# Narrow pieces of an attention row maximum: a plain maximum on VectorE, with the mask added on TensorE

## The chip, the cores and the metric

The kernel runs on one core of a Trainium2 chip. The metric is the device time of one execution in microseconds (us), taken as the median of several runs. The engines named below are TensorE (PE in the profile, its weight loads PEld), VectorE (DVE), ScalarE (ACT), GpSimd (POOL) and the DMA queue of SyncE (SP).

## The reference

The computation is one transformer layer over x of shape 4 x 1024 x 256, with a context of 77 rows per batch element placed in front of the keys. Attention has 16 heads of 16 numbers, and a query may see the whole context and the x rows up to its own:

```
xc = concatenate((mem, layernorm(x)))          # 77 + 1024 = 1101 keys
q, k, v = heads(layernorm(x) @ Wq), heads(xc @ Wkv)
dots = (q @ k.T) * 16 ** -0.5
dots = where(key > query + 77, -inf, dots)     # the triangle
x = x + softmax(dots) @ v @ Wout + bout
x = x + ffn(layernorm(x))                      # 256 -> 1024 -> gelu -> 256, block-quantized operands
```

The softmax is computed with the largest score of each row subtracted, so that row maximum has to be known before the exponentials. Everything in this document is about how that maximum is found.

## The kernel before

The 64 pairs of batch element and head are worked off in 16 groups `kk` of four heads. Within a group the four heads c = 0 to 3 lie in four bands of 32 partitions of the tiles `qTs` and `kTs`. A band holds the 16 numbers of the head, and one row more, into which the negated row maximum is written, so that the matmul of scores subtracts it by itself.

Each group passes through two phases, and the phases of neighbouring groups are interleaved: while the scores of group kk are computed, turned into exponentials and multiplied by v, the row maxima of group kk + 1 are found. The unit of this interleaving is `half_step(kk, n, pair)`. In it TensorE does two matmuls for the maxima (`max_matmul`, L523, into a tile of the pool `ps_s`, which has three buffers) and two for the scores (`score_matmul`, L587, into `ps_st`, two buffers), alternating, each on its own band of 32 rows of the array, so that they run beside each other. The trace shows each of these float32 matmuls as two passes, so that such a block has eight rows. Then VectorE takes the maxima of the two tiles (`max_reduce`), and ScalarE takes the exponentials (`score_exp`, L598). After the half-step come the products with v of an earlier step (`times_v`, L624), and then the units of other work (layer norm, projections, the feed-forward part, loads) which a planner by prices and due times fits in. All engines work off their instructions in the order in which they were written, and the three `ps_s` buffers are shared by the maxima and all those units: a matmul that needs a buffer waits until VectorE or ScalarE has read what was in it.

The keys that a tile of 128 queries can see are cut into pieces (`max_pieces`). For query tile `it` there are 77 + 128 (it + 1) keys. The widths of the pieces, in the order in which they are worked off, are

| query tiles | pieces by width |
|---|---|
| it 0 to 3 | 512 (it 3), 461 (it 2), 333 (it 1), 205 (it 0), 77 (it 3) |
| it 4 to 7 | 512 (it 4, 5, 6, and two of it 7), 461 (it 6), 333 (it 5), 205 (it 4), 77 (it 7) |

A piece that ends at the tile's own last key is diagonal: its last 128 columns hold the triangle. The pieces of 205 columns are diagonal, those of 77 are not. `max_reduce` has two forms. A first piece that is not diagonal is read by `tensor_reduce` (L547). Every other piece is read by a custom operation (`tensor_tensor_reduce`, L549; CUSTOM_DVE_ANT_0 in the profile). It adds a mask from the float32 tile `tri` (zeros, or the triangle in the last 128 columns), takes the maximum, starting from the result `mx` of the row's earlier piece where there is one, and writes the sums to a scrap tile `jk`. It is followed by a short instruction that reads out the result (DVE_READ_ACCUMULATOR2_ANT). For a piece of 77 columns the mask is all zeros.

The results are columns of the tile `mxp`, one tile for even and one for odd groups. `put_max` transposes it (L557) and sends it through DRAM into the maximum row of `qTs`, once for each half of the query tiles. Group 0 has no earlier group beside it: `first_step` does the maxima of its four heads at once, two of them in a `ps_st` tile.

Of the kernel before, what the change touches and what calls it, by code (L numbers as in the profile page):

```python
# [9 lines left out]
F32 = mybir.dt.float32  # L10
BF16 = mybir.dt.bfloat16
I32 = mybir.dt.int32
AF = mybir.ActivationFunctionType
ALU = mybir.AluOpType
AX = mybir.AxisListType
PSUM = bass.MemoryType.PSUM

P = 128
HEADS = 16
HD = 16  # L20
PAD = 32
HPC = P // HD
MXR = 1
HPG = 4
NG = HEADS // HPG
ICW = 512
# [17 lines left out]
def kernel(  # L44
# [14 lines left out]
    nc = tc.nc  # L59
    B, N, D = x.shape  # L60
    M = mem.shape[1]
    HID = w_fc.shape[0]
    NT = N // P
# [8 lines left out]
    const = ctx.enter_context(tc.tile_pool(name="const", bufs=1))  # L72
    small = ctx.enter_context(tc.tile_pool(name="small", bufs=4))
# [9 lines left out]
    for w, src in ((wk_sb, wkv[:, 0:D]), (wq_sb, wq), (wv, wkv[:, D : 2 * D]), (wo_sb, wout)):  # L83
# [6 lines left out]
    ZW = ICW - P  # L90
    tri = const.tile([P, ICW], F32, name="tri")
# [2 lines left out]
        out=tri[:, ZW:], in_=tri[:, ZW:], compare_op=ALU.is_ge, fill=NEG, base=0,  # L94
        pattern=[[-1, P]], channel_multiplier=1,
    )
    ones3 = const.tile([3, P], BF16, name="ones3")
    nc.gpsimd.memset(ones3, 1.0)

# [3 lines left out]
    identb = const.tile([P, P], BF16, name="identb")  # L103
# [126 lines left out]
    with ExitStack() as actx:  # L230
        ap = lambda name, bufs, **kw: actx.enter_context(tc.tile_pool(name=name, bufs=bufs, **kw))
        keep = ap("keep", 1)
# [13 lines left out]
        junk = ap("junk", 4)  # L246
# [18 lines left out]
            "q": keep.tile([P, N], F32, name="q_st"), "k": keep.tile([P, KEYS], F32, name="k_st")  # L265
        }
        mxps = [keep.tile([P, 2 * HPG * NT // 2], F32, name=f"mxp{i}") for i in range(2)]
        for i in range(2):
            nc.gpsimd.memset(mxps[i], 0.0)
        for i in range(2):  # L270
            nc.gpsimd.memset(qTs[i], 0.0)
        zero = keep.tile([P, 1], F32, name="zero")
# [18 lines left out]
        def s_tile(shape, dtype=F32):  # L291
            return ps_s.tile(shape, dtype, tag="s", name="s_ps")
# [206 lines left out]
        def max_pieces():  # L499

            pieces = []
            for half in range(NIC):
                some = []
                for it in range(half * ICW // P, (half + 1) * ICW // P):
                    n = M + (it + 1) * P
                    full, left = divmod(n, ICW)

                    lo = left if left < P else 0  # L510
                    cuts = [(lo + i * ICW, lo + (i + 1) * ICW) for i in range(full)]
                    if left:
                        cuts.append((0, left) if lo else (n - left, n))
                    some += [(it, *c, i, len(cuts)) for i, c in enumerate(cuts)]
                pieces += sorted(some, key=lambda p: p[1] - p[2])
            return pieces

        mxs = {}

        def max_matmul(kk, piece, c, sp):  # L520
            it, lo, hi, _, _ = piece
            rows = slice(c * PAD, (c + 1) * PAD)
            nc.tensor.matmul(  # L523
                sp[:, 0 : hi - lo], qTs[kk % NQK][rows, it * P : (it + 1) * P],
                kTs[kk % NQK][rows, lo:hi],
                start=True, stop=True,
            )

        def max_reduce(kk, piece, c, sp):
            it, lo, hi, i, many = piece  # L530
            w = hi - lo
            if i == 0:
                before = -3.0e38
            else:
                before = mxs[kk, it, c][:, i - 1 : i]
            if i == many - 1:
                col = (it // 4 * HPG + c) * 4 + it % 4
                into = mxps[kk % 2][:, col : col + 1]
            else:
                if i == 0:  # L540
                    mxs[kk, it, c] = small.tile([P, 2], F32, name="mx", bufs=6 * HPG)
                into = mxs[kk, it, c][:, i : i + 1]
            diagonal = hi == M + (it + 1) * P
            assert diagonal or w <= ZW or i == 0
            mask = tri[:, ICW - w : ICW] if diagonal else tri[:, 0:w]
            if i == 0 and not diagonal:
                nc.vector.tensor_reduce(into, sp[:, 0:w], axis=AX.X, op=ALU.max)  # L547
            else:
                nc.vector.tensor_tensor_reduce(  # L549
                    junk.tile([P, ICW], BF16, name="jk")[:, 0:w], sp[:, 0:w], mask, 1.0, before, ALU.add, ALU.max, into  # L550
                )

        def put_max(kk, half):


            mt = small.tile([P, PAD], F32, name="mt")
            nc.vector.transpose(mt, mxps[kk % 2])  # L557
            NQ, NI = P // PAD, ICW // P
            md = dram.tile([NQ, 2, HPG, NI, PAD], F32, name="md")
            nc.sync.dma_start(out=md.rearrange("q f c i j -> (q f c i) j"), in_=mt)  # L560
            nc.sync.dma_start(
                out=qTs[kk % NQK][MXR:P:PAD, half * ICW : (half + 1) * ICW].rearrange(
                    "c (i q j) -> c i q j", q=NQ, j=PAD
                ),
                in_=md[:, half].rearrange("q c i j -> c i q j"),
            )
# [16 lines left out]
        def score_matmul(kk, n, c, st, e):  # L583
            t, ic, i0, i1 = PIECES[n]
            nj = min(P, KEYS - t * P)
            rows = slice(c * PAD, (c + 1) * PAD)
            nc.tensor.matmul(  # L587
                st[:nj, e, : i1 - i0], kTs[kk % NQK][rows, t * P : t * P + nj],
                qTs[kk % NQK][rows, i0:i1],
                start=True, stop=True,  # L590
            )

        def score_exp(kk, n, pair, st):
            t, ic, i0, i1 = PIECES[n]
            nj = min(P, KEYS - t * P)
            w = i1 - i0
            pt = ptp.tile([P, 2, ICW], F32, name="pt")
            nc.scalar.activation(pt[:nj, :, :w], st[:nj, :, :w], AF.Exp, scale=scale)  # L598

            base = i0 - (t * P - M)  # L600
            behind = min(w, nj - 1 - base)
            if behind > 0:
                nc.gpsimd.affine_select(  # L603
                    out=pt[:nj, :, :behind], in_=pt[:nj, :, :behind], compare_op=ALU.is_ge,
                    fill=0.0, base=base, pattern=[[0, 2], [1, behind]], channel_multiplier=-1,
                )
            pts[kk, n, pair] = pt
# [321 lines left out]
        MAXP = max_pieces()  # L929
# [67 lines left out]
        def first_step(n):  # L997

            st = ps_st.tile([P, 2, ICW], F32, name="st_ps")
            tops = [s_tile([P, ICW]), s_tile([P, ICW]), st[:, 0, :], st[:, 1, :]]  # L1000
            for c, sp in enumerate(tops):
                max_matmul(0, MAXP[n], c, sp)
            for c, sp in enumerate(tops):
                max_reduce(0, MAXP[n], c, sp)

        def half_step(kk, n, pair):

            other = 1 - pair
            tops, st = [], None
            has_max, has_main = kk + 1 < B * NG, kk >= 0  # L1010
            if has_main:
                st = ps_st.tile([P, 2, ICW], F32, name="st_ps")
            for e in range(2):
                if has_max:
                    tops.append(s_tile([P, ICW]))
                    max_matmul(kk + 1, MAXP[n], pair * 2 + e, tops[e])
                if has_main:
                    score_matmul(kk, n, other * 2 + e, st, e)
            for e, sp in enumerate(tops):
                max_reduce(kk + 1, MAXP[n], pair * 2 + e, sp)  # L1020
            if has_main:
                score_exp(kk, n, other, st)
# [10 lines left out]
        def run(kk, extras):  # L1033
# [10 lines left out]
            for n in range(STEPS):  # L1044
                for pair in range(2):
                    if kk == last:
                        if pair == 0:
                            last_step(kk, n)
                    elif kk >= 0:
                        half_step(kk, n, pair)  # L1050
                    elif pair == 0:
                        first_step(n)
# [5 lines left out]
                    if n == 1 and pair == 0 and kk >= 0:  # L1058
                        put_max(kk, 1)
                    if n == HALF_AT + 2 and pair == 0 and kk + 1 < B * NG:  # L1060
                        put_max(kk + 1, 0)
# [31 lines left out]
        for kk in range(last + 1):  # L1093
            b, g = divmod(kk, NG)
            f = b - 1
# [35 lines left out]
            else:  # L1131
                n = -(-len(w_units) // NG)
# [60 lines left out]
```

## Time and profile before

| what | value |
|---|---|
| median of three runs | 1026.15 us (1023.31 to 1030.79) |
| time of the profiled execution | 1026.0 us |
| its span, first to last instruction | 1024.3 us |
| mean granted TensorE clock in it | 0.962 |
| busy: PE, PEld, DVE, ACT, POOL | 958.9, 406.9, 651.7, 564.9, 363.2 us |

The span is cut into 40 slices in the profile, and PE is busy in 90% or more of each from the third to the 37th. The clock was granted in full from 60 us to 905 us, but for a rounding. A busy time of PE is a union of pipelined instructions whose ends are modelled, so it is read together with the starts of the instructions in the timeline. A row of a group of instructions gives line, engine, operation, tiles written and read, shapes, count, then busy time and the mean of one instruction in ns, then the idle time of the engine in front of them and what ended it.

### The profile page before, as it was taken

The numbers are of one execution on the slowest core, as the hardware profiler recorded it, in microseconds if no ns is written. First come the engines' busy times: TensorE is split into PE (matmuls) and PEld (weight loads), VectorE is DVE, ScalarE is ACT, GpSimd is POOL, SyncE is SP. The second block draws the span as 40 slices with busy tenths as digits, with TensorE's granted clock in tenths as the row PEclk, the third lists the DMA queues.
The fourth block names the chain that finished last, engine by engine and source line by source line (L and its number), as shares of the span: only waits on it lengthen the run. The fifth ranks groups of instructions, "written<-read, shape, count | busy, mean of one in ns | idle before, by whom it ended". The sixth has DMA issues, their size and how long they took to land.

```text
span 1024.3 us, 21081 instructions
## 1 busy us (share of the span) xinstructions
PE 958.9 (94%) x8015; PEld 406.9 (40%) x8024; DVE 651.7 (64%) x2131; ACT 564.9 (55%) x838; POOL 363.2 (35%) x763
## 2 busy tenths in 40 slices
PE   4899999999999999999999999999999999999477
PEld 2343434344444343334443444334443444344133
DVE  4586776677667565647567475646558486662696
ACT  4234665555555655666555665665555665766134
POOL 1011323041435254333625244434425246342133
PEclk9899999999999999999999999999999999989566
DMA  3012000401021001200121001100122000002100
GB/s 106 23 54 67 10 29 8 112 14 40 27 70 26 17 10 36 80 7 27 31 69 38 19 15 36 40 7 16 32 66 58 12 13 14 17 8 74 47 21 21
DMA packets 36172, 36.31 MB, mean 35 GB/s; under 512 B 14067, under 2 KB 29747, under 8 KB 36070
## 3 DMA queue, kind: packets, MB, share of 16 engines
q1 hardware_dynamic: 34958, 33.90, 12.0%
q8 instruction: 63, 1.03, 0.4%
q10 hardware_dynamic: 1112, 1.06, 0.3%
q14 instruction: 39, 0.32, 0.1%
HBM read 16.58 MB, written 5.25 MB: 21 GB/s over the span
## 4 chain that ended last, share of the span: by engine, by line
PE 79%; DVE 11%; ACT 3%; DMA 2%; issue 2%; POOL 1%; SPq 1%; POOLq 0%; DVEq 0%; ACTq 0%
PE s_ps L523 33%; PE av_ps L624 16%; PE s_ps L446 6%; PE st_ps L587 5%; DVE jk L549 4%; PE st_ps L810 3%; PE s_ps L417 3%; PE s_ps L725 3%; PE s_ps L870 2%; PE st_ps L815 2%; DVE mx L547 1%; PE s_ps L862 1%; ACT pt L598 1%; DVE amaxh L183 1%; ACT h L821 1%
## 5 line engine op out<-in xcount | busy, mean ns | idle before, releaser
L598 ACT ACTIVATE pt<-st_ps 128x1024 f32<-128x1024 f32 (+4 forms) x448 | 353.2, 793 | 261.6 <-PE st_ps L587 237.4
L523 PE MATMUL s_ps<-kT,qT 32*128 32x512 f32 (+2 forms) x1736 | 481.1, 529 | 13.4 <-DVE mxp L549 5.8
L587 PE MATMUL st_ps<-qT,kT 32*128 32x512 f32 (+5 forms) x1792 | 472.8, 526 | 3.3 <-ACT pt L598 3.0
L603 POOL TENSOR_SCALAR_AFFINE_SELECT pt<-pt 128x254 f32<-128x254 f32 (+3 forms) x320 | 118.0, 371 | 422.8 <-ACT pt L598 422.1
L523 PEld LDWEIGHTS s_ps<-kT,qT 32*128 32x128 f32 x1736 | 188.4, 184 | 188.9 <-issue 66.1
L549 DVE CUSTOM_DVE_ANT_0 jk<-s_ps,tri,mx 128x77 bf16<-128x77 f32 (+3 forms) x372 | 174.0, 505 | 90.2 <-PE st_ps L587 58.8
L624 PE MATMUL av_ps<-pt,vaug 128*32 128x256 f32 (+7 forms) x3072 | 221.1, 362 | 2.1 <-issue 0.6
L547 DVE TENSOR_REDUCE mx<-s_ps 128x1 f32<-128x512 f32 x248 | 159.3, 684 | 88.5 <-PE st_ps L587 84.5
L549 DVE CUSTOM_DVE_ANT_0 jk<-s_ps,tri 128x512 bf16<-128x512 f32 (+3 forms) x248 | 126.9, 549 | 130.6 <-PE st_ps L587 95.7
L587 PEld LDWEIGHTS st_ps<-qT,kT 32*128 32x128 f32 (+1 forms) x1792 | 182.2, 181 | 12.9 <-ACT pt L598 9.4
L624 PEld LDWEIGHTS av_ps<-pt,vaug 128*32 128x32 f32 (+1 forms) x3072 | 61.9, 108 | 190.7 <-issue 128.2
L206 POOL TENSOR_TENSOR hq<-h,magh 128x512 bf16<-128x512 f32 x64 | 68.7, 1077 | 32.9 <-DVE h L205 29.8
L205 POOL TENSOR_TENSOR h<-h,magh 128x512 f32<-128x512 f32 x40 | 41.9, 1049 | 53.7 <-DVE magh L194 53.7
L821 ACT ACTIVATE h<-st_ps 128x1024 f32<-128x1024 f32 x32 | 32.8, 1025 | 30.3 <-PE st_ps L815 30.2
L183 DVE TENSOR_REDUCE amaxh<-h 128x16 f32<-128x512 f32 x64 | 42.7, 677 | 8.9 <-ACT h L821 8.9
L710 ACT COPY y<-s_ps 128x256 f32<-128x256 f32 x64 | 23.9, 374 | 42.9 <-PE s_ps L729 22.5
L810 PE MATMUL st_ps<-wfcT,xqT 128*128 128x512 bf16 x119 | 41.5, 428 | 3.1 <-ACT xqT L791 2.9
L549 DVE DVE_READ_ACCUMULATOR2_ANT mxp<- 128x1 f32 x512 | 42.1, 82 | 0.0
L417 PE MATMUL s_ps<-wv,xT 128*128 128x256 f32 (+1 forms) x144 | 40.8, 409 | 0.3 <-ACT vaug L422 0.3
L446 PE MATMUL s_ps<-xT,wk_sb 128*128 128x512 f32 (+1 forms) x96 | 38.8, 532 | 0.0
L870 PE MATMUL s_ps<-wprT,hT 128*128 128x256 bf16 x256 | 35.8, 286 | 3.2 <-ACT hT L865 2.6
L725 PE MATMUL s_ps<-wo_sb,o_pk 128*128 128x256 f32 x128 | 38.8, 429 | 0.0
(105 smaller groups left out, 797.7 us busy)
## 6 DMA issues: line engine op xcount, KB each, us to landing
kT<-k_st SPq DMA_DIRECT2D x16, 275.2 KB
xn<-in_x_dram SPq DMA_DIRECT2D x16, 256.0 KB
qT<-q_st SPq DMA_DIRECT2D x16, 256.0 KB
o_pk<-o_st SPq DMA_DIRECT2D x32, 128.0 KB
rb<-rd SPq DMA_DIRECT2D x128, 32.0 KB
x<-in_x_dram SPq DMA_DIRECT2D x32, 128.0 KB
out_dram<-x SPq DMA_DIRECT2D x32, 128.0 KB
x<-in_L_ffn_w_fc_dram SPq DMA_DIRECT2D x8, 128.0 KB
```

The costliest lines, as they stand in the source:

```text
L206: nc.gpsimd.tensor_tensor(dst.rearrange("p (n k) -> p n k", k=QBLK), src3, magb, ALU.subtract)
L417: nc.tensor.matmul(vp[:nj, :], xT[b][:, k, jt * P : jt * P + nj], wv[:, k, :], start=(k == 0), stop=(k == KC - 1),)
L446: nc.tensor.matmul(pp[:, :n], w[:, k, hi * P : (hi + 1) * P], xT[b][:, k, first + lo : first + lo + n], start=(k == 0), stop=(k == KC - 1),)
L523: nc.tensor.matmul(sp[:, 0 : hi - lo], qTs[kk % NQK][rows, it * P : (it + 1) * P], kTs[kk % NQK][rows, lo:hi], start=True, stop=True,)
L547: nc.vector.tensor_reduce(into, sp[:, 0:w], axis=AX.X, op=ALU.max)
L549: nc.vector.tensor_tensor_reduce(junk.tile([P, ICW], BF16, name="jk")[:, 0:w], sp[:, 0:w], mask, 1.0, before, ALU.add, ALU.max, into)
L587: nc.tensor.matmul(st[:nj, e, : i1 - i0], kTs[kk % NQK][rows, t * P : t * P + nj], qTs[kk % NQK][rows, i0:i1], start=True, stop=True,)
L598: nc.scalar.activation(pt[:nj, :, :w], st[:nj, :, :w], AF.Exp, scale=scale)
L603: nc.gpsimd.affine_select(out=pt[:nj, :, :behind], in_=pt[:nj, :, :behind], compare_op=ALU.is_ge, fill=0.0, base=base, pattern=[[0, 2], [1 ...
L624: nc.tensor.matmul(acc[c * PAD : (c + 1) * PAD, off + lo : off + hi], vaugs[b % 2][:nj, t, v0 : v0 + PAD], pts[kk, n, c // 2][:nj, c % 2, ...
L725: nc.tensor.matmul(yp, o_pk[b, ic][:, k, it * P % ICW : it * P % ICW + P], wo_sb[:, k, :], start=(k == 0), stop=False,)
L810: nc.tensor.matmul(hp[:, n, :], xqT[t][:, k, :], wfcT[:, k, n * ICW : (n + 1) * ICW], start=(k == 0), stop=False,)
```

## The change

Pieces under 256 columns (those of 205 and of 77) are read by `tensor_reduce` in place of the custom operation. Since `tensor_reduce` adds no mask, a new function `max_mask` lets TensorE add the triangle to the last 128 columns of a diagonal narrow piece: a bf16 matmul of the identity with `trib`, a bf16 copy of the triangle, which accumulates into the tile that `max_matmul` filled. It stands behind all matmuls of the half-step. Pieces of 77 columns get no mask.

The maximum of a narrow piece no longer starts from that of the row's other piece. It goes into its own column of a new tile `mxn` (where it is the row's only piece, it 0, into `mxp`), and `put_max` takes the larger of `mxp` and `mxn` with one operation on 16 columns before it transposes. The custom operation stays for the diagonal pieces of 333, 461 and 512 columns. The order of all other instructions on every engine's queue stays as it was.

```diff
+    trib = const.tile([P, P], BF16, name="trib")
+    nc.vector.tensor_copy(trib, tri[:, ZW:])
...
+        mxns = [keep.tile([P, 2 * HPG * NT // 2], F32, name=f"mxn{i}") for i in range(2)]
         for i in range(2):
             nc.gpsimd.memset(mxps[i], 0.0)
+            nc.gpsimd.memset(mxns[i], -3.0e38)
...
+        NARROW = 256
+
+        def masked(piece):
+            it, lo, hi, _, _ = piece
+            return hi == M + (it + 1) * P and hi - lo < NARROW
+
+        def max_mask(piece, sp):
+            it, lo, hi, _, _ = piece
+            if masked(piece):
+                nc.tensor.matmul(
+                    sp[:, hi - lo - P : hi - lo], identb, trib, start=False, stop=True,
+                    skip_group_check=True,
+                )
+
         def max_reduce(kk, piece, c, sp):
             it, lo, hi, i, many = piece
             w = hi - lo
...
+            col = (it // 4 * HPG + c) * 4 + it % 4
+            into, beside = (m[kk % 2][:, col : col + 1] for m in (mxps, mxns))
             diagonal = hi == M + (it + 1) * P
...
+            if w < NARROW:
+                assert masked(piece) or not diagonal
+                nc.vector.tensor_reduce(
+                    beside if many > 1 else into, sp[:, 0:w], axis=AX.X, op=ALU.max
+                )
+                return
+            wide = [p for p in MAXP if p[0] == it and p[2] - p[1] >= NARROW]
+            i = [p[1] for p in wide].index(lo)
+            if i < len(wide) - 1:
+                mxs[kk, it, c] = small.tile([P, 1], F32, name="mx", bufs=6 * HPG)
+            target = into if i == len(wide) - 1 else mxs[kk, it, c]
...
         def put_max(kk, half):
+            part = slice(half * PAD // 2, (half + 1) * PAD // 2)
+            nc.vector.tensor_tensor(
+                mxps[kk % 2][:, part], mxps[kk % 2][:, part], mxns[kk % 2][:, part], ALU.max
+            )
             mt = small.tile([P, PAD], F32, name="mt")
             nc.vector.transpose(mt, mxps[kk % 2])
...
         def half_step(kk, n, pair):
...
+            for sp in tops:
+                max_mask(MAXP[n], sp)
             for e, sp in enumerate(tops):
                 max_reduce(kk + 1, MAXP[n], pair * 2 + e, sp)
```

## The prediction

> **What bounds the kernel now.** I read the engines' totals first, then the slices, then the chain that ended last. All three stand on the profile's page.
>
> ```profile
> PE 958.9 (94%) x8015; PEld 406.9 (40%) x8024; DVE 651.7 (64%) x2131; ACT 564.9 (55%) x838; POOL 363.2 (35%) x763
> ...
> PE   4899999999999999999999999999999999999477
> ...
> PE 79%; DVE 11%; ACT 3%; DMA 2%; issue 2%; POOL 1%; SPq 1%; POOLq 0%; DVEq 0%; ACTq 0%
> ```
>
> PE is the bound: its 65 us without work lie mostly at the two ends, and the slices from the third to the 37th, where nearly all maxima are found, are full. VectorE is 11% of the chain, so here and there PE does wait for it. The view of waits says where: PE's weight loads for the maxima (L523) wait for VectorE to give back a buffer.
>
> ```profile
> PEld s_ps L523 <- DVE mxp L549: 46.1, 119, 1.7
> PEld s_ps L523 <- DVE mx L547: 28.1, 61, 1.0
> PEld s_ps L523 <- DVE mx L549: 12.9, 31, 0.8
> ```
>
> That is 87 us over 211 waits, but other bands often work meanwhile. What is lost I read from the timeline as the time from a block's first matmul to the next work. A block with nothing to wait for takes 0.56 us at 205 columns and 0.38 at 77; over all 62 and 63 blocks of these widths the means are 0.66 and 0.54. So the narrow blocks lose 62 x 0.10 + 63 x 0.16 = 16 us in all. This is the most that faster narrow maxima could give back in their own steps.
>
> **The masks on TensorE.** Groups 1 to 15 have their maxima in half-steps; each has four half-steps of 205 columns (two query tiles, two pairs), each with two masks: 60 pairs, 120 matmuls. Group 0 has two steps with four masks. Before shows no mask, but it shows a near twin: L788 turns two 128 x 128 bf16 tiles with the same identity, each with its own weight load. In the timeline of TensorE:
>
> ```profile
> 330.78 0.28 PE L788 MATMUL s_ps<-identb,xq 128*128 128x128 bf16 x2
> 331.00 0.54 PE L523 MATMUL s_ps<-kT,qT 32*128 32x333 f32 x1
> ...
> 336.22 0.44 PE L523 MATMUL s_ps<-kT,qT 32*128 32x205 f32 x1
> ...
> 336.77 0.60 PE L624 MATMUL av_ps<-pt,vaug 128*32 128x231 f32 x8
> ...
> 363.95 0.62 PE L862 MATMUL s_ps<-identb,hq 128*128 128x128 bf16 x8
> 364.50 0.69 PE L523 MATMUL s_ps<-kT,qT 32*128 32x512 f32 x1
> ```
>
> The pair holds TensorE 0.215 us from its start to the next block's (0.22 here; 0.215 is the commonest over all such pairs), eight hold it 0.55 us. The slope is (0.55 - 0.215) / 6 = 0.056 us a matmul, and 0.10 us is paid once, for going from the full array back to bands. A block of 205 columns takes its 0.56 us before the products with v, and blocks in front of full-array work take no longer (1.07 us at 512 columns before L870 as before L624), so a mask pair between them adds the whole 0.215. Sixty pairs are 12.9 us; group 0's two sets are 2 x (4 x 0.056 + 0.10) = 0.65. Sum: **+13.5 us**, on the engine that sets the end. Bounds: 128 x 0.056 = 7 us if the change of kind is free, since both neighbours pay for it already; and 13.5 + 128 x 0.10 = 26 us if each weight load is laid bare (0.10 us is the mean of L862's and L788's loads). I take the pair as measured; the accumulation into a filled bank is new, but L810, which accumulates too, shows no gap for it.
>
> The Trainium skill, "TensorE: Matmul & The Clock Gate", section "Back-to-back issue gap", gives 134 cycles at 2.4 GHz, 56 ns, for an isolated matmul of 128 columns; the slope agrees, and by this alone 128 masks would be 7.2 us. The 0.10 us for the change of kind is not in that formula, and for it the rows decide.
>
> **The narrow maxima on VectorE.** The rows by shape, and two stretches of VectorE's timeline:
>
> ```profile
> L547 DVE TENSOR_REDUCE mx<-s_ps 128x1 f32<-128x512 f32 x248 | 159.3, 684 | 88.5 <-PE st_ps L587 84.5 <-PE st_ps L523 2.7 <-PE s_ps L523 0.5
> L549 DVE CUSTOM_DVE_ANT_0 jk<-s_ps,tri,mx 128x77 bf16<-128x77 f32 x124 | 32.2, 295 | 27.8 <-PE s_ps L523 21.1 <-PE st_ps L587 5.5
> L183 DVE TENSOR_REDUCE amaxx<-xh 128x8 f32<-128x256 f32 x32 | 13.2, 413 | 0.0
> ```
>
> ```profile
> 494.41 0.43 DVE L549 CUSTOM_DVE_ANT_0 jk<-s_ps,tri,mx 128x205 bf16<-128x205 f32 x1
> 494.76 0.08 DVE L549 DVE_READ_ACCUMULATOR2_ANT mxp<- 128x1 f32 x1
> ...
> 517.32 0.30 DVE L549 CUSTOM_DVE_ANT_0 jk<-s_ps,tri,mx 128x77 bf16<-128x77 f32 x1
> 517.54 0.08 DVE L549 DVE_READ_ACCUMULATOR2_ANT mxp<- 128x1 f32 x1
> ...
> 519.02 1.29 DVE L547 TENSOR_REDUCE mx<-s_ps 128x1 f32<-128x512 f32 x2 [0.71 <-PE st_ps L587]
> ```
>
> The custom operation and the reading of its result overlap the next one: what counts is the step from start to start, 0.35 us for 205 columns that start from mx (494.41 to 494.76), 0.29 us for 205 without it, and 0.22 us for 77. Two plain maxima of 512 columns take 1.29 us, each alone 0.68, so their step is 0.61. The plain maximum costs (677 - 413) / 256 = 1.03 ns a column (L183 at 512 and at 256 columns), which puts its step at 0.61 - 435 x 0.00103 = 0.16 us for 77 columns and 0.29 us for 205. So VectorE gains 128 x 0.06 for the 77s, 64 x 0.06 for it 4, and nothing for it 0: 11.5 us. The bounds are no gain at all, if the step has a floor at the 0.22 of the custom one, and 256 x 0.08 = 20 us, if every reading of a result (82 ns) went in full. `put_max` gets 32 operations on 16 columns, and the transpose waits for each: the small operations of L162 stand 0.20 us apart, so +6.4 us, between 32 x 0.17 and 32 x 0.40. The balance is some -5 us of VectorE's 652.
>
> How much reaches PE? Sorted by what they wait for, about half of the narrow blocks' 16 us goes to VectorE working off a queue that other work has lengthened (statistics, quantization), the rest mostly to ScalarE and GpSimd. In some 20 such blocks the shorter maxima (two to four in front of the waiting matmul, 0.06 each) give back about 0.15 us each: -3 us. In another nine or so PE would have waited anyway behind a mask pair, for ScalarE or GpSimd, and the pair fits in: -2 us. Against this, `put_max` falls into the steps of 461 and 512 columns, where PE waits for VectorE most; I let a sixth of its 6.4 us through: +1 us. Sum: **-4 us**, between -16 (all waits of narrow blocks gone) and +6 (nothing gained, all of `put_max` let through).
>
> The Trainium skill speaks against the new operation: "VectorE: DVE Perf Modes", section "Rules for kernel authors", calls tensor_reduce the slowest VectorE operation. Here it takes 684 ns at 512 columns against 689 to 748 for the custom one, so the rule does not hold for this pair; by it the gain would be nothing, which is the lower bound above.
>
> **What costs nothing.** The copy into `trib` stands first on VectorE and waits for GpSimd's triangle (2.19 us); its successors feed ScalarE at 4.17 us, and the first statistics start at 4.53, so it has 1.9 us of cover, and without it would cost at most 0.5. The two extra fills of `mxn` on GpSimd are 0.09 us each, far ahead of any reader. A masked maximum now waits for the mask, 0.1 to 0.2 us later; behind it on VectorE wait the other maximum and the planner's operations, but the products with v (0.53 us) stand on PE in between before the buffer is asked for, and they move along. ScalarE waits for the scores, which stand ahead of the masks. The transfers of `put_max` start 0.2 us later; the only DMA wait on L523 is for group 0's qT.
>
> **The forecast.** 1026.0 (profiled execution; the median is 1026.15, no difference that matters) + 13.5 - 4 = **1035.5**, 0.9% slower. A change under 1%, 10 us, can hardly be told from none here.
>
> **Rivals.**
> - *The masks' price as measured, small relief* (1030 to 1041): chance 0.5.
> - *VectorE really was the narrow steps' bound*: the masks cost only their columns (+7) and all 16 us of narrow waits go: 1017, range 1012 to 1029, chance 0.15. For it: 211 waits on VectorE. Against: most of them stand at 333 to 512 columns, and VectorE idles before most blocks of 205. It ends faster than before if the waits given back exceed the masks' price; at the measured price that takes 13.5 of the 16.
> - *The identity's weights are not loaded beside the blocks in bands*, as the full array's are needed at once: 26 - 4 = +22, 1048, range 1041 to 1054, chance 0.2. It decides once a mask pair holds PE over 0.3 us. Against: L788's loads, 0.10 us each, hide within the 0.215 us.
> - *The plain maximum is no faster when narrow* (the change doesn't do what it is for): +13.5 for the masks, +1 for `put_max`, and only the 2 us of masks that fit into waits come off: 1038.5, range 1037 to 1042, chance 0.15. It decides if a step at 77 columns stays at 0.22 us.
>
> Faster by over 1% comes from the second alone (0.06). Slower by over 1% takes 0.2 of the first, 0.2 of the third and nearly 0.1 of the last: 0.48. Within 1% keeps 0.46. For the range, 1024 to 1046 leaves out about a tenth on each side.
>
> **What would show it.** In the profile after: 128 more bf16 matmuls of 128 columns, with 0.2 to 0.23 us from the first of a pair to the products with v; plain maxima of about 235 ns at 77 columns and 370 at 205; 223 fewer VectorE instructions (256 readings of results go, 33 operations come); narrow blocks losing about 11 us in place of 16; PE's busy time up by about 10 us. I am wrong if the pair takes 0.11 or 0.4 us, or if the waits on VectorE at 333 to 512 columns, which I take as untouched, change by more than some 5 us.

## The result, and the profile after

The changed kernel took 1039.97 us (median of six runs, 1033.16 to 1042.74) against 1027.94 us for the kernel before (six runs): a ratio of 1.0108, 95% interval 1.0064 to 1.0152. Run once more beside other kernels, it came to 1.0084 (1.0050 to 1.0118). Ratios here and below leave out executions over 1.5% longer than the fastest of their kernel (three of the eight of the kernel with the masks alone, none elsewhere), and are therefore given in place of differences of medians. The forecast was 1035.5 us, or +9.5 us over the profiled execution of before; the two comparisons make it +11 and +9.

The profiled execution took 1042.27 us, with a span of 1040.5 us, 16.3 us more than before's. Its page, in the parts that were shown of before (totals, slices of PE and of its clock, the chain that ended last):

```profile
PE 976.6 (94%) x8143; PEld 414.0 (40%) x8152; DVE 646.1 (62%) x1908; ACT 565.2 (54%) x838; POOL 362.6 (35%) x765
...
PE   4899999999999999999999999999999999998568
...
PEclk9899999999999999999999999989999999989565
...
PE 78%; DVE 12%; ACT 2%; issue 2%; DMA 2%; POOL 1%; SPq 1%; POOLq 0%; DVEq 0%; ACTq 0%
```

PE is as full as before and has 128 matmuls more; VectorE has 223 instructions fewer and is busy 5.6 us less. The new thing is the 8 in the 27th slice of the clock, of which more below; the same row of before is

```profile
PEclk9899999999999999999999999999999999989566
```

A half-step of 205 columns with its masks, in TensorE's timeline:

```profile
518.72 0.44 PE L530 MATMUL s_ps<-kT,qT 32*128 32x205 f32 x1
...
519.36 0.29 PE L545 MATMUL s_ps<-trib,identb 128*128 128x128 bf16 x2
519.57 0.60 PE L652 MATMUL av_ps<-pt,vaug 128*32 128x230 f32 x8
```

From the first mask of a pair to the products with v it is 0.21 us in these rounded rows; by the starts in ns it is 216 to 218 in each of the 60 pairs. The two sets of four in group 0 take 0.33 us each. So the masks add 60 x 0.217 + 2 x 0.33 = 13.7 us to TensorE's stream. And the narrow maxima, in VectorE's timeline, and then two rows of the groups by shape:

```profile
522.00 0.65 DVE L559 TENSOR_REDUCE mxp<-s_ps 128x1 f32<-128x205 f32 x2 [1.72 <-PE s_ps L545]
522.56 0.42 DVE L146 BATCH_NORM_STATS2 st<-xn 128x6 f32<-128x256 f32 x1
523.01 0.18 DVE L147 BATCH_NORM_AGGREGATE mv<-st 128x2 f32<-128x6 f32 x1
523.11 0.35 DVE L559 TENSOR_REDUCE mxn<-s_ps 128x1 f32<-128x77 f32 x2
523.76 0.38 DVE L559 TENSOR_REDUCE mxn<-s_ps 128x1 f32<-128x77 f32 x2 [0.30 <-PE st_ps L615]
```

```profile
L559 DVE TENSOR_REDUCE mxn<-s_ps 128x1 f32<-128x77 f32 x124 | 23.9, 230 | 32.0 <-PE s_ps L530 23.8 <-PE st_ps L615 7.8
L559 DVE TENSOR_REDUCE mxp<-s_ps 128x1 f32<-128x205 f32 x62 | 20.1, 366 | 40.9 <-PE s_ps L545 40.8
```

Two maxima of 205 columns take 0.65 us and one 0.366, so the step from start to start is 0.28 us in these rows (287 to 289 ns by most of the starts); at 77 columns it is 0.38 - 0.23 = 0.15. The bracket of the first row, like the last column of the L559 row of 205 columns, names the mask as what VectorE now waits for.

In terms of blocks (the time from a block's first matmul to the next work, over the time it takes with nothing to wait for), the loss is as follows:

| blocks of | 512 | 461 | 333 | 205 | 77 columns |
|---|---|---|---|---|---|
| before, us lost | 43.8 | 21.1 | 18.7 | 6.4 | 9.6 |
| after, us lost | 42.7 | 21.2 | 21.0 | 6.2 | 6.1 |

The column of 512 takes the half-steps of groups 1 to 15, with 1.07 us as the time of a block that waits for nothing; the other columns take all blocks. The narrow blocks lose 3.7 us less, the wide ones 1.3 us more (3.8 more in a second trace of the change). How far the after trace lags behind can be read at each of the 32 transposes of `put_max`, the same instruction in both: 0.2 us at the second, then growing steadily to 8.9 at the 24th, 11.9 at the 25th and 12.9 at the last. The rise of 3.0 us within one step stands where the clock fell. Behind the last maxima another 3.4 us are added, in a part of the program that the change does not touch; there too it is most likely the clock, granted at 0.71 from 914 us to the end, against 0.75 from 901 us to the end before: over the ten traces of this case the part behind the last transpose takes 119.9 to 124.3 us, and roughly the longer the more of it ran at half the clock (59 to 75 us). The account of the 16.3 us is thus, roughly: masks 13.7, narrow blocks -3.7, the clock's fall in the loop about 3, the last part 3.

### The profile page after: what moved, and what is told of

Same layout as the page of the kernel before. It is cut to its first block, busy times and chain, and to the rows that moved or that the text cites. A ratio compares the mean times of both kernels' runs of the same rounds, so it can differ in the third digit from the quotient of the medians.

```text
span 1040.5 us, 21096 instructions
## 1 busy us (share of the span) xinstructions
PE 976.6 (94%) x8143; PEld 414.0 (40%) x8152; DVE 646.1 (62%) x1908; ACT 565.2 (54%) x838; POOL 362.6 (35%) x765
## 3 DMA queue, kind: packets, MB, share of 16 engines
q1 hardware_dynamic: 34958, 33.90, 11.9%
q8 instruction: 64, 1.05, 0.4%
## 4 chain that ended last, share of the span: by engine, by line
PE 78%; DVE 12%; ACT 2%; issue 2%; DMA 2%; POOL 1%; SPq 1%; POOLq 0%; DVEq 0%; ACTq 0%
PE s_ps L530 32%; PE av_ps L652 16%; PE s_ps L451 6%; PE st_ps L615 5%; DVE jk L572 4%; PE s_ps L422 3%; PE st_ps L838 3%; PE s_ps L753 3%; PE s_ps L898 2%; PE st_ps L843 2%; DVE amaxh L185 1%; PE s_ps L890 1%; PE s_ps L545 1%; ACT pt L626 1%; DVE mx L570 1%
## 5 line engine op out<-in xcount | busy, mean ns | idle before, releaser
L530 PE MATMUL s_ps<-kT,qT 32*128 32x512 f32 (+2 forms) x1736 | 479.3, 530 | 14.5 <-DVE mxp L572 7.5
L530 PEld LDWEIGHTS s_ps<-kT,qT 32*128 32x128 f32 x1736 | 185.9, 184 | 189.5 <-issue 57.6
L615 PEld LDWEIGHTS st_ps<-qT,kT 32*128 32x128 f32 (+1 forms) x1792 | 180.1, 182 | 12.0 <-ACT pt L626 8.8
L572 DVE CUSTOM_DVE_ANT_0 jk<-s_ps,tri 128x512 bf16<-128x512 f32 (+2 forms) x186 | 106.0, 608 | 96.4 <-PE st_ps L615 61.2
L570 DVE TENSOR_REDUCE mx<-s_ps 128x1 f32<-128x512 f32 x186 | 119.6, 683 | 51.0 <-PE st_ps L615 47.8
L572 DVE CUSTOM_DVE_ANT_0 jk<-s_ps,tri,mx 128x512 bf16<-128x512 f32 (+2 forms) x186 | 117.1, 669 | 42.9 <-PE st_ps L615 42.0
L559 DVE TENSOR_REDUCE mxn<-s_ps 128x1 f32<-128x77 f32 (+1 forms) x186 | 44.0, 275 | 59.6 <-PE s_ps L545 27.5
L570 DVE TENSOR_REDUCE mxp<-s_ps 128x1 f32<-128x512 f32 x62 | 40.0, 687 | 37.2 <-PE st_ps L615 36.2
L207 POOL TENSOR_TENSOR h<-h,magh 128x512 f32<-128x512 f32 x40 | 41.9, 1047 | 54.5 <-DVE magh L196 54.5
L185 DVE TENSOR_REDUCE amaxh<-h 128x16 f32<-128x512 f32 x64 | 42.7, 677 | 10.3 <-ACT h L849 10.3
L559 DVE TENSOR_REDUCE mxp<-s_ps 128x1 f32<-128x205 f32 x62 | 20.1, 366 | 40.9 <-PE s_ps L545 40.8
```

The source lines that it names most:

```text
L530: nc.tensor.matmul(sp[:, 0 : hi - lo], qTs[kk % NQK][rows, it * P : (it + 1) * P], kTs[kk % NQK][rows, lo:hi], start=True, stop=True,)
L559: nc.vector.tensor_reduce(beside if many > 1 else into, sp[:, 0:w], axis=AX.X, op=ALU.max)
L570: nc.vector.tensor_reduce(target, sp[:, 0:w], axis=AX.X, op=ALU.max)
L572: nc.vector.tensor_tensor_reduce(junk.tile([P, ICW], BF16, name="jk")[:, 0:w], sp[:, 0:w], tri[:, ICW - w : ICW], 1.0, mxs[kk, it, c] if i ...
L615: nc.tensor.matmul(st[:nj, e, : i1 - i0], kTs[kk % NQK][rows, t * P : t * P + nj], qTs[kk % NQK][rows, i0:i1], start=True, stop=True,)
```

## The experiments

Each kernel ran beside the kernel before on the same chip, in two groups of four on two chips. The traces allow a comparison that the clock disturbs less. From the third to the last transpose of `put_max` the clock was granted in full but for some falls to half. The time between the two, times the clock granted in it, is the time that the stretch would have taken at the full clock; before it is 811.2 us. The stretch holds 58 of the 60 mask pairs, 58 x 0.217 = 12.6 us.

| kernel | ratio to before | stretch at the full clock, against before |
|---|---|---|
| the change | 1.0108 | +8.4 us |
| the change once more | 1.0084 | +8.4 us |
| the masks alone | 1.0107 | +9.3 us |
| without the masks | 0.9960 | -2.6 us |
| every mask twice | 1.0141 | +16.4 us |
| comparison with one operand | 1.0068 | +8.2 us |
| without the masks, comparison with one operand | 0.9943 | -2.0 us |
| only 77 columns plain | 0.9969 | -2.1 us |
| all pieces plain, no triangle | 0.9919 | -6.9 us |

The two traces of the change agree. But a stretch at half the clock is counted as exactly half the work here, and the lag behind before shifts by up to 0.8 us where the clock falls, so that differences under about 1 us say nothing.

**The masks alone**, on the kernel before:

```diff
+            for sp in tops:
+                max_mask(MAXP[n], sp)
             for e, sp in enumerate(tops):
                 max_reduce(kk + 1, MAXP[n], pair * 2 + e, sp)
```

> The kernel before with the 128 masks of the change added on TensorE; all maxima stay with the custom operation (the triangle is then added twice to the narrow diagonal pieces, which changes no maximum), no combination in put_max. If the masks are paid in full on TensorE (217 ns a pair in the profile after): +13 us against before, and no relief elsewhere, so some +12 to +13.5. If the masks fit into waits that are there anyway, and the change's loss comes from put_max or the clock: +5 to +9.

Measured: 1.0107 of before (1.0064 to 1.0151), 11 us, and the mask pairs at 216 to 218 ns again. This is a little under the first theory's +12, and the interval, whose lower end is +6.6, reaches into the second's range, so it favours the first theory without excluding the second. The trace is between the two: 9.3 us of the 12.6 are paid, and some 3 fit into waits. The next kernel shows that put_max and the clock are not the loss.

**The change without its masks:**

```diff
         def max_mask(piece, sp):
             it, lo, hi, _, _ = piece
-            if masked(piece):
-                nc.tensor.matmul(
-                    sp[:, hi - lo - P : hi - lo], identb, trib, start=False, stop=True,
-                    skip_group_check=True,
-                )
+            return
```

> The changed kernel without its masks: a narrow diagonal piece is then read with the triangle left out, so that the row's largest score may be too large; the softmax subtracts it all the same. If the masks are the loss: what is left is the relief of the narrow blocks (3.7 us less lost in them in the profile after) less what put_max's new operation costs, so -4 to 0 us against before. If put_max or the clock are the loss: +3 us or more.

Measured: 0.9960 (0.9934 to 0.9985), 4 us under before; 2.6 us by the table above. Without the masks the loss is gone, and a small gain is left; the masks are the loss. Taking them out also ends VectorE's wait for them, but the blocks of 205 columns and those of 77 behind them lose no more with the masks than before (6.2 and 6.1 us against 6.4 and 9.6), so it is TensorE's time that they cost. The narrow blocks lose 14.5 us in its trace, 1.5 less than before, against 3.7 less with the masks: by this count the faster maxima by themselves give back 1.5 us in their own steps, and the other 2.2 us are waits in which the masks found room.

**Every mask twice:**

```diff
-            for sp in tops:
+            for sp in tops + tops:
                 max_mask(MAXP[n], sp)
```

> The changed kernel with every mask issued twice, behind each other (the triangle added twice, no other maximum). By the slope of the prediction, 56 ns a mask and 0.10 us once for the change of kind: four masks hold TensorE 0.33 us in place of 0.217, and the time is 60 x 0.112 + 0.4 = 7 us above the change. If the price belongs to each mask (0.11 us, weight load included): +13 us above the change. If masks hide: less than +4.

Measured: 1.0141 (1.0111 to 1.0171), some 3 to 6 us above the change by the two ratios of the change, with intervals that overlap. The trace is sharper than the ratio: the table has 8.0 us more than for the change, where 58 x 0.113 = 6.6 were to come. In TensorE's timeline four masks stand between the block and the products with v:

```profile
528.55 0.40 PE L545 MATMUL s_ps<-trib,identb 128*128 128x128 bf16 x4
528.88 0.60 PE L652 MATMUL av_ps<-pt,vaug 128*32 128x230 f32 x8
```

They hold TensorE 0.330 us in each of the 60 half-steps, 0.113 us more than two. So the price is 0.056 us a mask and 0.10 us once; each mask's own weight load (98 ns) is hidden. What the 0.10 us is paid for can be seen in before, where the same pair of L788 stands ahead of a block in bands, and also ahead of a bf16 matmul over the full array:

```profile
433.92 0.28 PE L788 MATMUL s_ps<-identb,xq 128*128 128x128 bf16 x2
434.13 0.33 PE L523 MATMUL s_ps<-kT,qT 32*128 32x77 f32 x1
...
435.92 0.28 PE L788 MATMUL s_ps<-identb,xq 128*128 128x128 bf16 x2
436.04 0.38 PE L810 MATMUL st_ps<-wfcT,xqT 128*128 128x512 bf16 x1
```

It holds TensorE 0.216 us by the starts in ns in the first case and 0.122 in the second. Ahead of a float32 matmul over the full array (L725, at 796 us) it is 0.213. So the 0.10 us is paid when the next work is of another kind, in bands or float32, and not only for the step back to bands that the prediction names; which part of the change costs it is not shown.

**The comparison in `put_max` by an operation with one operand:**

```diff
-            nc.vector.tensor_tensor(
-                mxps[kk % 2][:, part], mxps[kk % 2][:, part], mxns[kk % 2][:, part], ALU.max
+            nc.vector.tensor_reduce(
+                mxps[kk % 2][:, part], mxqs[kk % 2][:, part, :], axis=AX.X, op=ALU.max
             )
```

> The changed kernel with the two pieces of a row compared by a tensor_reduce over two neighbouring columns (one operand in SBUF) in place of a tensor_tensor of two tiles. In the profile after three of the 32 tensor_tensor lasted 0.97 to 1.05 us, each to the end of a GpSimd tensor_tensor (L207), and behind one of them TensorE stood still and its clock fell to half for 6.8 us. If GpSimd holds that operation because of its two operands: no combination over 0.35 us, and 1 to 4 us less than the change, 1036 to 1039. If it was chance or the hold concerns any operation there: as slow as the change, with holds of 1 us.

Measured: 1.0068 (1.0045 to 1.0090), 1.6 to 4 us under the two ratios of the change. What the ratio cannot quite settle the traces do. In the changed kernel, by time over all engines (rows picked; then TensorE's):

```profile
692.64 1.05 POOL L207 TENSOR_TENSOR h<-h,magh 128x512 f32<-128x512 f32 x1
...
692.75 0.97 DVE L581 TENSOR_TENSOR mxp<-mxp,mxn 128x16 f32<-128x16 f32 x1
...
693.75 0.21 DVE L585 STREAM_TRANSPOSE mt<-mxp 128x32 f32<-128x32 f32 x1
...
694.55 0.81 PE L530 MATMUL s_ps<-kT,qT 32*128 32x333 f32 x1 [0.83 <-DVE mxp L572]
```

An operation on 16 columns, 0.168 us as a rule, lasts 0.97 us and ends 0.03 us after GpSimd's: it was held. VectorE's next maxima are late by that, and TensorE stands still for 0.83 us for a buffer. Behind the other two holds, at 391 and 629 us, TensorE has a projection of 1.9 us (L451) to do and does not stand still. With the tensor_reduce, in the trace of this experiment, the same meeting goes by unnoticed:

```profile
688.19 1.05 POOL L207 TENSOR_TENSOR h<-h,magh 128x512 f32<-128x512 f32 x1
...
688.30 0.18 DVE L581 TENSOR_REDUCE mxp<-mxq 128x16 f32<-128x32 f32 x1
```

Three of the 32 comparisons are held for about 1 us in every trace of the tensor_tensor form (the change twice, the one without masks, the one with masks twice), always behind L207; in the form with one operand three also start in the first 0.11 us of an L207, and none of the 32 lasts over 0.183 us. So the second operand is what the hold needs. That the time gains by it is not shown: the ratios overlap, and at the full clock the stretch is only 0.2 us shorter than with the change. One transpose after the first hold (at the 15th of 32) the two traces of the change lag behind before by 3.9 and 4.0 us, counted from the third transpose, and this form by 3.9.

**The change once more**, in the second group:

> The changed kernel once more, beside the three below on one chip: 1.011 of before, as in the first comparison (1.0064 to 1.0152), with three or so operations in put_max of 1 us. A ratio under 1.006 would mean that the first comparison caught much of the clock's scatter.

Measured: 1.0084 (1.0050 to 1.0118), and three comparisons of about 1 us again. The first result stands, perhaps a little high.

**Without masks and with the comparison by tensor_reduce** (both edits above):

> The changed kernel without the masks (the row's largest score may then be too large; the softmax subtracts it all the same) and with the two pieces of a row compared by a tensor_reduce. If masks and the held operation are two separate losses: the 0.4% by which the kernel without masks alone beat before, and 2 to 3 us more, 0.992 to 0.995 of before. If the hold cost nothing: 0.996.

Measured: 0.9943 (0.9910 to 0.9975), inside the range for two separate losses; but the step from 0.9960 is within the intervals, and the table does not have it (-2.0 us against -2.6), so that the second gain is not shown. Against the kernel that differs from it by the masks alone (1.0068, on the other chip), the masks cost 1.25%, 12.9 us; their price in the traces is 13.7 less the 2.2 us that fit into waits, and by the table 10.2 of 12.6 (11.0 with the comparison held).

**Only the pieces of 77 columns plain:**

```diff
-        NARROW = 256
+        NARROW = 128
```

> The changed kernel with the bound of a narrow piece at 128 columns in place of 256, and the comparison by tensor_reduce: only the pieces of 77 columns, which hold no triangle, are read by the plain maximum; those of 205 stay with the custom operation and there is no mask; the computation is whole. If the relief comes from the 77s (step from start to start 0.16 us in place of 0.22), and the 205s give next to nothing (0.29 in place of 0.29 and 0.35): as fast as the kernel without masks and with tensor_reduce, within 2 us; 0.992 to 0.997 of before. If the relief is the 205s': 0.998 to 1.002.

Measured: 0.9969 (0.9935 to 1.0003), at the edge of the first expectation's range, 2.7 us by the ratios above the kernel in which the 205s are plain too, where 2 were allowed, and with an interval that reaches into the second's range. The traces settle what the ratio does not: at the full clock the stretch is 2.1 us shorter than before's, with the 205s plain too 2.0. So the relief is that of the 77s, as the first theory has it.

**All pieces plain, no triangle, one comparison of two or three columns:**

```diff
-            if w < NARROW:
...
-                nc.vector.tensor_tensor_reduce(
...
+            nc.vector.tensor_reduce(
+                mxqs[kk % 2][:, col, i : i + 1], sp[:, 0:w], axis=AX.X, op=ALU.max
+            )
```

> All pieces read by the plain maximum, no triangle anywhere in the maxima (the row's largest score may be too large; the softmax subtracts it all the same), a row's two or three pieces compared by one tensor_reduce over neighbouring columns. 192 custom operations that start from an earlier result (0.67 us from start to start at 512 columns) become 0.61: 11 us less on VectorE in the wide steps, where TensorE loses some 68 us in blocks. If these losses follow VectorE's load: 3 to 6 us under the kernel in which only the narrow pieces are plain, 0.987 to 0.991 of before. If they come from the planner's other work: no more than 1 us.

Measured: 1021.04 us, 0.9919 (0.9890 to 0.9948), 2.5 us by the ratios under the kernel in which only the narrow pieces are plain, with intervals that overlap, and 4.9 us by the table, inside the first theory's 3 to 6. So the wide steps do follow VectorE's load. Its rows by shape:

```profile
L550 DVE TENSOR_REDUCE mxq<-s_ps 128x1 f32<-128x512 f32 x372 | 239.2, 684 | 166.1 <-PE st_ps L592 131.7 <-PE s_ps L530 31.7 <-PE st_ps L530 1.7
L550 DVE TENSOR_REDUCE mxq<-s_ps 128x1 f32<-128x461 f32 x124 | 73.3, 630 | 24.9 <-PE st_ps L592 23.4 <-PE st_ps L530 1.2 <-PE s_ps L530 0.4
```

The wide blocks lose some 3 us less in this trace than before, and the narrow ones 1.8 less. (The 68 us of the expectation for the wide blocks before are 84 by the table of blocks above, with its time for a free block of 512 columns.) This version beats both kernels, the one before by 8 us and the changed one by 17. It rests on a property of the computation: the softmax is the same whatever is subtracted in a row, so the maximum may include keys behind the triangle. The kernel then has the same result as long as no score behind the triangle exceeds the allowed ones by so much that the exponentials vanish. How near the data here come to that was not measured.

## Why the prediction was right

- **What bounds the kernel.** Right: work added to TensorE's stream came out at the end. Of 12.6 us of masks in the stretch of the table 9.3, 10.2 and 11.0 are paid, by the three pairs of kernels that differ in the masks.
- **The masks.** Predicted 0.215 us a pair and +13.5 us in all, measured 0.217 and 13.7. The near twin, L788, carried over to a matmul that accumulates. The bounds, 7 and 26 us, were never near; the doubled masks confirm the slope of 0.056 and the 0.10 paid once, though the surroundings of L788 show that it is not paid for bands alone.
- **The narrow maxima.** The durations were right (predicted 235 and 370 ns, measured 230 and 366; steps of 0.16 and 0.29 us, measured 0.15 and 0.29). Their effect on TensorE was forecast at -3 us. In their own blocks it is -1.5; the stretch of the table gains 2.0 to 2.6 us without the masks, with `put_max`'s operation in it, which is what -3 and +1 make together. The single terms cannot be told apart at this size. The -2 us for masks that fit into waits is -2.2 by the narrow blocks, and between -1.6 and -3.3 by the table.
- **The comparison in `put_max`.** +1 us was expected from its 32 x 0.20 us. The usual length was right (0.168), but three were held for 0.8 to 0.9 us more by GpSimd, 2.6 us of VectorE in all, in the steps of 461 and 333 columns. What reaches the end of that is not shown: 2 to 4 us by the ratios, whose intervals overlap, and nothing clear of 1 us at the full clock. The prediction has no term for a second engine that holds VectorE; if the hold cost little, that was the luck of the projections behind two of the three.
- **What would show it.** 223 fewer VectorE instructions, as predicted. The narrow blocks lose 12.3 us, predicted 11. One sign came out against the prediction: the waits of the maxima's weight loads (L523) for VectorE at 333 to 512 columns were 70.5 us before and are 76.3 and 78.2 in the two traces of the change, which is more than the 5 us allowed. With the comparison by tensor_reduce they are 73.2, so half of it or more comes with the holds. As blocks the wide steps lose 1.3 and 3.8 us more, for other bands work meanwhile, and the sum held. PE's busy time rose by 17.7 us and not by 10: it also counts the time in which the clock was lower. From the third to the 23rd transpose, where the clock fell in neither trace, it rose by 6.6 us in 20 of the 31 steps between transposes, which would make 10 in all.
- **The sum.** The forecast of +9.5 us met +11 and +9 in the ratios. The ratios' own intervals are 7 to 9 us wide, so an agreement this close is in part luck; the stretch at the full clock, +8.4 us with two pairs of masks and those of group 0 outside it, says the same.
- **The rivals.** VectorE as the bound of the narrow steps is refuted by the kernel without masks, which gains 4 us (2.6 by the table) in place of the 16 of the narrow waits. Weights that are not loaded beside the blocks are refuted by the pairs' 217 ns, and a plain maximum that is no faster when narrow by its step of 0.15 us.

## What to carry to other kernels

When an operation is moved off an engine that is not the bound and onto one that is, price it on the second with the nearest twin in the trace, from its start to the start of the next kind of work; the change between kinds (0.10 us here) can cost as much as the work. Before a mask is moved at all, ask whether the value needs it: a shift that the softmax cancels may be too large without harm, and leaving the mask out gained more than either way of adding it here. A small operation with two operands in SBUF can meet one of GpSimd; with one operand it was not held here, though that did not measurably shorten the whole.

## What the runs showed of the hardware

**VectorE held by GpSimd.** The meeting shown above was not expected. The Trainium skill, "SBUF — State Buffer", section "SBUF: two separate sides", describes a pair of ports that VectorE, for an operation with two SBUF inputs, and GpSimd share: whichever starts first has it for its whole instruction. The traces agree in the main: comparisons with two inputs that start 0.03 to 0.10 us into an L207 of 1.05 us end 0.03 us after it, and those with one input do not wait. But one that starts 0.92 us into an L207 takes its usual 0.17 us and ends ahead of it; the ends of GpSimd's instructions are rough in the trace.

**The clock inside the loop.** The forecast takes over the clock of before, which fell to half twice for 3.4 us at 66 and 77 us and was then full until the last maxima, at 906 us. In the changed kernel it fell to half for 6.8 us just behind TensorE's wait of 0.83 us. The stretches of the trace, with the granted clock behind the engines' busy times:

```profile
60.00:690.00 630.00, 617.06 (x5385) 256.61 (x5390) 398.05 (x1207) 363.67 (x543) 225.74 (x517) 0.99 0.13 36
690.00:694.00 4.00, 3.71 (x28) 1.35 (x24) 3.83 (x14) 1.96 (x3) 1.94 (x4) 1.00 0.00 0
694.00:702.00 8.00, 7.45 (x35) 3.14 (x36) 2.93 (x12) 2.71 (x5) 4.01 (x6) 0.57 0.07 20
```

It did so again at the same place, 693 us, when the change was profiled a second time. But in the kernel without masks and in that with masks twice the comparison at this place was held too, and the clock stayed full there; and without any hold it fell for 3.4 to 6.8 us at other places (at 453 us in the trace of the comparison by tensor_reduce, at 446 us in that of all plain pieces). The kernel with the masks alone, which has no comparison, fell at the same step of the program as the change, at 710 us. That the hold sets it off is therefore not shown. The places recur, however: seven of the ten traces have a fall between the 16th and the 17th transpose, those of before and of the change do not. All these falls last a multiple of 3.4 us.

**How far the clock scatters the time.** In 33 executions of the unchanged kernel on the second chip the time went from 1022.03 to 1037.21 us. On the first chip, where each of 19 has its mean clock beside it, 1025.3 us goes with 0.961 and 1035.6 us with 0.950. A difference of 3 us between two kernels is thus smaller than what the clock does to one of them, and it was read from the traces, at the same instruction in each, and not from the times alone.
